# A selective-scan layer: shared products for B and C, paired input norm, centring folded into sums, and new rules for background work

## The chip, the core and the metric

The program runs on one core of a Trainium2 chip. A core has TensorE (PE, matrix products), VectorE (DVE), ScalarE (ACT), GpSimd (POOL) and a queue for DMA issues on SyncE (SP). The metric is the device time of one execution in microseconds (us); lower is better. A DMA moves data between HBM and the on-chip memory SBUF. PE writes to PSUM, a second on-chip memory of which this kernel gives two banks to small products.

## The reference, cut to what matters

Four layers follow one another; only the first is changed. It works on 8 images of 64 channels and 64 x 64 places. The part that matters:

```python
# x: (B, 64, 64, 64); DI = 128, N = 16, R = 4, K = 4 directions
xh = xh + _ss2d(_ln(xh, ln1_g, ln1_b), ...)      # norm over the 64 channels
xz = einsum(x, in_proj_w) + in_proj_b            # 64 -> 2 * 128
xi, z = split(xz, 2)
xc = silu(dwconv3(xi))                           # 3 x 3, per channel
xs = stack(rows of xc, columns of xc, both of them reversed)   # k = 0, 1, 2, 3
dts, Bs, Cs = split(einsum(xs, xproj_w), [R, R + N])
dts = softplus(dts through dtproj_w + dtproj_b)
h = h * exp(dt * A) + dt * B * u                 # for each of 16 n, along L = 4096
y_k = sum over n of h_n * C_n  + D * u
y = y_0 + y_1 + y_2 + y_3                        # put back in place
y = _ln(y, outnorm_g, outnorm_b) * silu(z)       # norm over the 128 channels
x = x + y through outproj_w
```

Directions 0 and 2 read the same places of xc, as do 1 and 3; they differ in their weights and in the direction of the scan.

## The kernel before, in words

**Steps and turns.** An image takes 16 steps: four directions by four chunks of 1024 places (`steps`, order k = 0, 2, 1, 3, for the last image 1, 3, 0, 2). A step takes 16 turns, one for each n, so 8 images make 2048 turns. In a turn, written out by hand under a manual schedule: ACT makes `a` (L628); DVE multiplies `z` by `dus` in PSUM (L673) and runs the scan (L677); POOL multiplies the scan's result with C into `ct` (L682); PE adds `ct` to the running sum in PSUM (`sum_up`, L719, a product with the identity), three turns behind. For n in `BY_POOL` = 0, 3, 6, 8 the product with B is made on POOL (L636) from a broadcast copy, and ACT copies it to PSUM (L643), so that DVE has only the scan. Otherwise PE spreads B over the partitions (`spread`, L646) from three bf16 parts. C, and B for four n, reach SBUF by broadcast DMAs of 512 KB (L624), issued one turn ahead for C, into five `ct` buffers.

**Step ends.** At turn 3 `begin_sum` (L710) starts the new step's sum with `u` or the stored `y`, at turn 7 two sums are made, and at turn 3 ACT copies the finished sum to `y` (`empty`, L692). For odd k the places are read in columns, so these reads are strided.

**Preparation of the next step** (`prepare`, `project`, `pieces`): for odd k ACT turns `u` into `ut` (L558); two products give B and C (`lower`, L514), ACT copies them (L522), a DMA stores them to HBM; two products give the step size (L532), with two ACT passes each (L540, L541); Exp and Ln follow at turns 6 and 7 (L546, L549), two additions and multiplications on POOL (L552, L571). B is fetched again, split in three bf16 parts by ACT and POOL (L585 to L595), stored, and loaded as `bs`. These seven `pieces` run at turns 7 to 13.

**Background.** All other work is cut in items, a pair (make, use): `before` takes one item in a turn and issues its PE part, `after` issues the rest one turn later. The queue holds, for image b: output norm and projection of image b - 1 (`after`), loads, input norm and projection of image b + 1 (`norm_items`, `before`), its gates (Silu of z, L406), and its convolutions (nine products for each block of 512 places, in seven items of which two are empty; L421, L430). The items of the next step go to the front of the queue. `before` takes nothing at turn 7, and for odd k at turn 4. At the last step of an image `bg.drain()` empties the queue; half of the next image's convolutions are held back (`rest`) and go in front of its first steps. In image 0 (`early`) and in the last three steps (`late`) up to three and two items go in a turn.

**Norms.** For each block of 512 places: a product with I - 1/p centres it (L296), ACT copies it back (L300) and squares it (L302), a product sums the squares (L309). The variances go through HBM to be spread over 128 partitions (fetch L326, root L329, reciprocal on DVE L332, back L337), a product spreads them (L346), DVE multiplies (L350), ACT applies gain and bias (L351). The input norm uses 64 partitions, the output norm 128.

Of the kernel before, what the change touches and what calls it, by code (L numbers as in the profile page):

```python
# [165 lines left out]
class Background:  # L166
# [4 lines left out]

    def __init__(self):
        self.queue, self.last, self.late = deque(), None, []

    def add(self, items, first=False):
        if first:
            self.queue.extendleft(reversed(items))
        else:
            self.queue.extend(items)
# [4 lines left out]
    def before(self, skip=False):  # L184
        self.now = None
        if self.queue and not skip:
            make, use = self.queue.popleft()
            self.now = (use, make() if make else None)
# [12 lines left out]

    def drain(self):
        while self.queue or self.last or self.late:
            self.before()
            self.after()


def scan_layer(cm, x_in, w, xh):

    tc, nc = cm.tc, cm.nc  # L210
    with ExitStack() as ctx:
# [9 lines left out]
        ln1_g, ln1_b = cm.column(w["ln1_g"], C, "ln1_g"), cm.column(w["ln1_b"], C, "ln1_b")  # L221
# [9 lines left out]
        win = cm.tile([C, 2, DI], "win")  # L231
        for i in range(2):
            through(win[:, i, :], w["in_proj_w"][i * DI : (i + 1) * DI])
        wout = cm.tile([DI, C], "wout")
        through(wout, w["outproj_w"])
        wx = cm.tile([DI, 4, R + 2 * N], "wx")
# [4 lines left out]
        for k in range(4):  # L241
            through(wx[:, k, :], w["xproj_w"][k])
# [24 lines left out]
        ln1 = cm.norm_consts(C, "ln1")  # L267
        lno = cm.norm_consts(DI, "lno")
# [16 lines left out]
        def norm_items(src, p, consts, g, b, blocks=range(NBK)):  # L285

            cen, avg = consts
            j0, nb = blocks[0], len(blocks)
            var = dr.tile([L], F32, name="vard", tag="vard")[: nb * BK]
            rs = dr.tile([L], F32, name="rsd", tag="rsd")[: nb * BK]  # L290
            sq, sm = {}, {}

            def centre(j):
                def make():
                    ps = bank("cps")
                    nc.tensor.matmul(ps[:p], cen, src[:, bass.ts(j, BK)], start=True, stop=True)  # L296
                    return ps

                def use(ps):
                    nc.scalar.copy(src[:, bass.ts(j, BK)], ps[:p])  # L300
                    sq[j] = work.tile([128, BK], F32, name="sq", tag="sq")
                    nc.scalar.activation(sq[j][:p], ps[:p], AF.Square)  # L302

                return make, use

            def variance(j):
                def make():
                    ps = bank("vps1")
                    nc.tensor.matmul(  # L309
                        ps[:1], avg[:, NBK - 1 : NBK], sq.pop(j)[:p], start=True, stop=True  # L310
                    )
                    return ps

                def use(ps):
                    t = work.tile([NBK, BK], F32, name="vrow", tag="rstd", bufs=1)
                    nc.scalar.copy(t[:1], ps[:1])
                    bg.later(lambda: nc.sync.dma_start(
                        var[bass.ts(j - j0, BK)].rearrange("(o n) -> o n", o=1), t[:1]
                    ))

                return make, use
# [17 lines left out]
            def apply(j):  # L339
                blk = bass.ts(j, BK)  # L340

                def make():
                    ps = bank("rps")

                    row = cm.ident[:nb, j - j0 : j - j0 + 1].to_broadcast([nb, p])
                    nc.tensor.matmul(ps[:p], row, sm["r"], start=True, stop=True)  # L346
                    return ps

                def use(ps):
                    nc.vector.tensor_tensor(src[:, blk], src[:, blk], ps[:p], ALU.mult)  # L350
                    nc.scalar.activation(src[:, blk], src[:, blk], AF.Identity, bias=b, scale=g)  # L351

                return make, use

            none = (None, None)
            out = [centre(j) for j in blocks[:2]]
            for j in blocks:
                out.append(variance(j))
                if j + 2 - j0 < nb:
                    out.append(centre(j + 2))  # L360
            out += [none, (None, fetch), none, (None, root), (None, invert), none, (None, back)]
            out += [none] + [apply(j) for j in blocks]
# [3 lines left out]
        FIRST = (range(3), range(3, 5), range(5, 8))  # L366

        def before(b):

            xn = io.tile([C, L], F32, name="xn", tag="xn", bufs=1)  # L370
# [6 lines left out]
            def load(j):  # L377
                return lambda _: nc.sync.dma_start(xn[:, bass.ts(j, BK)], xs[:, bass.ts(j, BK)])

            def project_in(j):  # L380
                def make():
                    ps = bank("xps")
                    nc.tensor.matmul(
                        ps, win[:, 0, :], xn[:, bass.ts(j, BK)], start=True, stop=True
                    )
# [10 lines left out]
            def gate(j):  # L396
                def make():
                    ps = bank("zps")
                    nc.tensor.matmul(
                        ps, win[:, 1, :], xn[:, bass.ts(j, BK)], start=True, stop=True  # L400
                    )
# [9 lines left out]
            def convolve(j):  # L411
# [17 lines left out]
                def use(_):  # L429
                    nc.scalar.activation(u[:, bass.ts(j, BK)], held[0], AF.Silu, bias=convb)  # L430

                if b == 0:
                    return [(part(0, 5), None), (part(5, 9), use)]
                if b == NB - 1:
                    return [
                        (part(0, 3), None), (part(3, 5), None), (part(5, 7), None),
                        (part(7, 9), use),
                    ]
                return [
                    (part(0, 2), None), (part(2, 4), None), (None, None), (part(4, 6), None),  # L440
                    (part(6, 8), None), (None, None), (part(8, 9), use),
                ]

            items = [[(None, load(j)) for j in range(NBK)]]
            for blocks in (FIRST if b == 0 else (range(NBK),)):
                items.append(norm_items(xn, C, ln1, ln1_g, ln1_b, blocks))
                items[-1] += [project_in(j) for j in blocks]
            return u, zd, items, [gate(j) for j in range(NBK)], [convolve(j) for j in range(NBK)]

        def after(b, y, zd, blocks=range(NBK)):  # L450
# [15 lines left out]
            def project_out(j):  # L466
# [7 lines left out]
                def use(po):  # L474
# [6 lines left out]
                    if j + 2 in blocks:  # L481
                        multiply(j + 2)
# [3 lines left out]
            def begin(_):  # L486
                for j in blocks[:2]:
                    multiply(j)

            items = norm_items(y, DI, lno, on_g, on_b, blocks)  # L490
            items.insert(-2, (None, lambda _: [load(j) for j in blocks[:3]]))
            items += [(None, begin), (None, None)]
            out = [[project_out(j), (None, None)] for j in blocks]
            return items + sum(out, [])[:-1]
# [8 lines left out]
        def project(u, k, c):  # L503
# [5 lines left out]
            bc = dr.tile([2 * N, CH], F32, name="bc", tag="bc")  # L509

            def lower(i):
                def make():
                    ps = bank("dps")
                    nc.tensor.matmul(  # L514
                        ps[: 2 * N].rearrange("p (a b) -> p a b", b=S), wx[:, k, R:],
# [4 lines left out]
                def use(ps):  # L520

                    nc.scalar.copy(e[: 2 * N, bass.ts(i, BK)], ps[: 2 * N])  # L522
                    bg.later(lambda: nc.sync.dma_start(
                        bc[:, bass.ts(i, BK)], e[: 2 * N, bass.ts(i, BK)]
# [31 lines left out]
            def turn():  # L556

                nc.scalar.copy(uo, ordered(u, k, c))  # L558
# [1467 lines left out]
```

## Time and profile before

| | us |
|---|---|
| three timed runs, median (lowest to highest) | 12572.19 (12557.06 to 12573.62) |
| the profiled execution | 12567.77 |
| its span, first to last instruction | 12566.0 |
| first scan starts, last scan starts | 98.2, 7255.1 |

So the changed layer takes the first 7260 us or so of the span. The starts of the scans (L677) in the trace give the time of each image: 955.2, 883.7, 880.7, 877.6, 879.2, 878.2, 903.4 and 901.3 us for images 0 to 7. The same starts give each step, as a mean over images 2 to 5:

| step | 0 | 1 | 2 | 3 | 4 | 5 | 6 | 7 |
|---|---|---|---|---|---|---|---|---|
| us | 58.6 | 53.8 | 51.8 | 51.8 | 54.3 | 58.1 | 53.6 | 52.3 |
| **step** | **8** | **9** | **10** | **11** | **12** | **13** | **14** | **15** |
| us | 51.9 | 55.6 | 53.7 | 56.0 | 59.3 | 55.7 | 55.7 | 56.8 |

A profile's busy time is the time in which an engine executes; an idle gap is put down to what ended last before it. In the views below `x` is a count, numbers after `|` are busy us, mean ns of one, and idle us ahead of it with its cause.

### The profile page before, as it was taken

To read this page: it belongs to the slowest core of one execution; us is meant where nothing else is said; L and a number is where in the kernel's file an instruction comes from. 1 tells how busy PE (TensorE), PEld (TensorE's weight loads), DVE (VectorE), ACT (ScalarE), POOL (GpSimd) and SP (SyncE) were. 2 spreads that over 40 slices of the span, in tenths; PEclk is the share of its full clock that TensorE was granted. 3 is DMA by queue.
4 is the path that set the end of the run, shared out by engine and by line. 5 is a ranking of instruction groups with operands and counts; after the bars stand their busy time and mean duration, and the time that the engine had idled before them with its cause. 6 is when DMAs were issued, how large, how long until landed. Compare 5 with 4: busy or idle time off the path is not lost. (4 is left out here: it accounts for less than half of the span.)

```text
span 12566.0 us, 122564 instructions
## 1 busy us (share of the span) xinstructions
PE 11561.6 (92%) x39403; PEld 4098.9 (33%) x39403; DVE 10385.0 (83%) x7362; ACT 7996.2 (64%) x10740; POOL 7424.1 (59%) x3638
## 2 busy tenths in 40 slices
PE   7899999999999999999998889999987778999999
PEld 2233233233232332332332222332324463333333
DVE  4999999999989999999899858768687685676767
ACT  4777677777776776777776536546456584555554
POOL 4999999999999999999899810000004490000000
PEclk8999999999999999999999989999998788999999
DMA  3666666666656656656566510000011110000000
GB/s 96 211 203 205 213 203 204 213 201 211 211 197 220 204 196 220 205 200 219 191 200 211 186 47 15 17 24 6 18 38 39 40 25 23 12 11 17 6 11 6
DMA packets 547044, 1562.30 MB, mean 124 GB/s; under 512 B 133040, under 2 KB 150096, under 8 KB 543824
## 3 DMA queue, kind: packets, MB, share of 16 engines
q1 hardware_dynamic: 546384, 1554.33, 37.6%
q8 instruction: 314, 5.14, 0.2%
q14 instruction: 346, 2.83, 0.1%
HBM read 1456.35 MB, written 88.87 MB: 123 GB/s over the span
## 5 line engine op out<-in xcount | busy, mean ns | idle before, releaser
L682 POOL TENSOR_TENSOR ct<-ct,h 128x1024 f32<-128x1024 f32 x2048 | 4796.0, 2359 | 456.2 <-DVE h L677 197.7
L719 PE MATMUL yps<-ct,ident 128*128 128x512 f32 x8192 | 4071.2, 626 | 4.6 <-POOL ct L682 4.6
L677 DVE TENSOR_TENSOR_SCAN h<-a,state,z 128x1024 f32<-128x1024 f32 x1536 | 3572.2, 2341 | 102.7 <-POOL ct L682 30.8
L1027 DVE TENSOR_TENSOR sum<-sum,ex 128x1024 f32<-128x1024 f32 x1920 | 2348.1, 1223 | 617.9 <-ACT ex L1020 481.2
L1020 ACT ACTIVATE ex<-sc 128x1024 f32<-128x1024 f32 x2048 | 1967.9, 1024 | 1359.8 <-PE sc L1015 1359.8
L628 ACT ACTIVATE a<-dt,amat 128x1024 f32<-128x1024 f32 x2048 | 2344.7, 1146 | 611.5 <-DVE h L677 606.9
L673 DVE TENSOR_TENSOR z<-z,e 128x1024 f32<-128x1024 f32 x1536 | 1866.5, 1215 | 391.1 <-PE z L646 240.2
L719 PEld LDWEIGHTS yps<-ct,ident 128*128 128x128 f32 x8192 | 1444.8, 192 | 2033.2 <-issue 1816.6
L1034 PE MATMUL av<-ex,v 128*64 128x512 f32 x8192 | 1950.0, 604 | 0.0
L1015 PE MATMUL sc<-q,k 16*128 16x512 f32 (+1 forms) x8192 | 1562.2, 623 | 4.2 <-ACT q L1008 3.1
L677 DVE TENSOR_TENSOR_SCAN h<-a,z 128x1024 f32<-128x1024 f32 x512 | 1162.7, 2282 | 101.6 <-ACT z L643 85.9
L646 PE MATMUL z<-bs,pick 48*128 48x512 bf16 x3072 | 941.6, 387 | 324.7 <-DVE h L677 290.0
L636 POOL TENSOR_TENSOR bt<-bt,e 128x1024 f32<-128x1024 f32 x512 | 1209.1, 2362 | 4.7 <-DMA bt<-bc 4.7
L1341 POOL TENSOR_TENSOR gt<-gt,pad 128x1024 f32<-128x1024 f32 x16 | 34.9, 2179 | 1572.0 <-ACT gt L1340 1492.7
L1034 PEld LDWEIGHTS av<-ex,v 128*64 128x64 f32 x8192 | 512.2, 136 | 1332.8 <-issue 1278.9
L1015 PEld LDWEIGHTS sc<-q,k 16*128 16x128 f32 (+1 forms) x8192 | 528.4, 184 | 1016.2 <-issue 977.3
L643 ACT COPY z<-bt 128x1024 f32<-128x1024 f32 x512 | 519.4, 1014 | 460.4 <-DVE h L677 237.7
L646 PEld LDWEIGHTS <-pick 48*128 48x128 bf16 x3072 | 180.1, 95 | 1592.7 <-issue 756.6
L421 PE MATMUL vps<-pad,convd 128*128 128x512 f32 x1152 | 540.6, 594 | 0.0
L1714 DVE RECIPROCAL r<-e 128x512 f32<-128x512 f32 x128 | 420.7, 3324 | 0.0
L1717 POOL TENSOR_TENSOR r<-r,half 128x512 f32<-128x512 f32 x128 | 162.6, 1270 | 361.6 <-issue 188.8
L664 ACT COPY state<-h 128x1 f32<-128x1 f32 x2048 | 359.4, 176 | 1.6 <-DVE h L677 1.6
(408 smaller groups left out, 10581.9 us busy)
## 6 DMA issues: line engine op xcount, KB each, us to landing
ct<-bc SPq DMA_DIRECT2D x2048, 512.0 KB
bt<-bc SPq DMA_DIRECT2D x512, 512.0 KB
x<-x SPq DMA_DIRECT2D x12, 2048.0 KB
bc<-e SPq DMA_DIRECT2D x256, 64.0 KB
zd<-z SPq DMA_DIRECT2D x64, 256.0 KB
z<-zd SPq DMA_DIRECT2D x64, 256.0 KB
x<-x SPq DMA_DIRECT2D x32, 512.0 KB
part<-x SPq DMA_DIRECT2D x128, 128.0 KB
```

The costliest lines, as they stand in the source:

```text
L421: nc.tensor.matmul(held[0].rearrange("p (r c) -> p r c", c=S), convd[:, t, :], pad[:, j * rows + dy : (j + 1) * rows + dy, dx : dx + S], s ...
L628: ctl["exp", n] = nc.scalar.activation(ctl["a", n], ctl["dt"], AF.Exp, scale=amat[:, ctl["k"], n : n + 1])
L636: nc.gpsimd.tensor_tensor(bt, bt, ctl["dus"], ALU.mult)
L646: nc.tensor.matmul(z[:, bass.ts(i, BK)], pick[:, n : n + 1].to_broadcast([3 * N, DI]), ctl["bs"][:, bass.ts(i, BK)], start=True, stop=True,)
L673: first = nc.vector.tensor_tensor(z, z, ctl["dus"], ALU.mult)
L677: nc.vector.tensor_tensor_scan(h[:, flip], a[:, flip], z[:, flip], 0.0 if state is None else state[:, n : n + 1], ALU.mult, ALU.add,)
L682: freed[at] = nc.gpsimd.tensor_tensor(ct, ct, h, ALU.mult)
L719: nc.tensor.matmul(ctl["ps"][:, bass.ts(i, BK)], cm.ident, ct[:, bass.ts(i, BK)], start=False, stop=(n == N - 1 and not ctl["turns"]),)
L1015: nc.tensor.matmul(sc[:, e, :], k[r : r + d, bass.ts(j, 128)], qs[i][r : r + d, :], start=True, stop=True,)
L1020: nc.scalar.activation(ex, sc, AF.Exp)
L1027: nc.vector.tensor_tensor(sums[i], sums[i], ex, ALU.add)
L1034: nc.tensor.matmul(avs[i][r, :], v[:, j, r], ex[:, e, :], start=(j == 0), stop=(j == TQ - 1))
```

## The change

- **B and C of two directions in one product.** `lower` is made only for k < 2, with 64 weight columns: those of k and of k + 2. Store, fetch and split handle both (tiles twice as wide); a step with k >= 2 only loads its `bs`.
- **Input norm of two blocks at once.** Even blocks lie on partitions 0 to 63 and odd ones on 64 to 127, so the norm has four pairs in place of eight blocks. `in_proj_w` is held twice.
- **Centring inside the sums.** From the last step of the third direction on, the running sum is made with I - 1/128 (`lno_cen`) in place of the identity, so `y` is stored centred and the output norm has no centring product or copy.
- **Convolutions one per step.** A convolution is a group of five items (four in image 7) without empty ones. In each step one group (two in image 6) may open when enough turns are left for it; its items alternate with the queue's. `finish` forces convolutions only where the next step needs them; the drain at the image's end and `rest` are gone.
- **Busy turns kept free.** At turns 3, 6, 7 and 8 no item with a product is taken.
- The output norm's multiplications (POOL) follow each block's `apply`, and its projections come without empty items between them. The turn of `u` for odd k is issued at the start of the step.

```diff
-    def before(self, skip=False):
+    def before(self, busy=False, slots=0):
         self.now = None
-        if self.queue and not skip:
-            make, use = self.queue.popleft()
+        src = None
+        if busy:
+            if not self.queue or self.queue[0][0]:
+                return
+        elif self.open:
+            if not self.first and (self.item or len(self.open) >= slots or not self.queue):
+                src = self.open
+        elif self.groups and self.credit and not self.first and slots >= len(self.groups[0]):
+            src = self.open = self.groups.popleft()
+            self.credit -= 1
+        if src is None and self.queue:
+            src = self.queue
+            self.first = max(0, self.first - 1)
+        self.item = src is not self.open
+        if src:
+            make, use = src.popleft()
             self.now = (use, make() if make else None)
...
+    def finish(self, b, count):
+
+        while self.done.get(b, NBK) < count:
+            self.credit = 1
+            self.before(slots=NBK)
+            self.after()
...
+            out = [centre(i) for i in pairs[:2]] + [none] * (2 - len(pairs[:2]))
+            for i in pairs:
+                out.append(variance(i))
+                if i + 2 in pairs:
+                    out.append(centre(i + 2))
+            out += chain
+            out += [apply(i) for i in pairs[:2]] + [none] * (2 - len(pairs[:2]))
+            for i in pairs:
+                out += [project_in(2 * i), project_in(2 * i + 1)]
+                if i + 2 in pairs:
+                    out.insert(-1, apply(i + 2))
...
+            out = [(None, lambda _: [square(j) for j in blocks[:2]]), none]
+            out += [variance(j) for j in blocks] + chain
+            out.insert(-2, (None, lambda _: [load(j) for j in blocks[:3]]))
+            out += [apply(j) for j in blocks[:2]]
...
-        FIRST = (range(3), range(3, 5), range(5, 8))
+        FIRST = (range(2), range(2, 3), range(3, 4))
...
-                return [
-                    (part(0, 2), None), (part(2, 4), None), (None, None), (part(4, 6), None),
-                    (part(6, 8), None), (None, None), (part(8, 9), use),
-                ]
+                cuts = (0, 5, 9) if b == 0 else (0, 3, 5, 7, 9) if b == NB - 1 else (0, 2, 4, 6, 8, 9)
+                parts = [(part(t0, t1), None) for t0, t1 in zip(cuts, cuts[1:])]
+                return parts[:-1] + [(parts[-1][0], use)]
...
-            items = [lower(0), lower(1), step_size(0), step_size(1)]
+            items = [step_size(0), step_size(1)]
+            if k < 2:
+                low["bc"] = dr.tile([2, 2 * N, CH], F32, name="bc", tag="bc", bufs=8)
+                items = [lower(0), lower(1)] + items
             if k % 2:
...
-                items.insert(0, (turn, None))
+                nc.scalar.copy(uo, ordered(u, k, c))
+                items.insert(0, none)
...
-            return [fetch, first, subtract, second, third, store, get]
+            return ([fetch, first, subtract, second, third, store] if ctl["k"] < 2 else []) + [get]
...
-                    ctl["ps"][:, bass.ts(i, BK)], cm.ident, ct[:, bass.ts(i, BK)],
+                    ctl["ps"][:, bass.ts(i, BK)], ctl["mat"], ct[:, bass.ts(i, BK)],
...
+            bg.finish(b, 2 * c + 2 if s < NCH and k == 0 else NBK)
...
+                mat=lno_cen if s >= 3 * NCH - 1 else cm.ident,
...
+                bg.done[b] = 0
+                bg.add([(None, lambda _: bg.groups.extend(deque(conv) for conv in convs))])
                 bg.add(gates)
-                now = NBK // 2 if b < NB - 1 else NBK
...
-                        bg.drain()
                         nxt = prepare(b + 1, 0)
-                        bg.add(sum(rest.pop(b + 1, []), []))
+                    bg.credit = 2 if b == NB - 2 else 1
+                    idle = () if early or late else (3, 6, 7, 8)
...
-                            skip = twice or (n == LAG + 2 and ctl["k"] % 2 == 1)
-                            bg.before(skip and not early and not late)
+                            bg.before(n in idle, slots)
```

## The prediction

> **What bounds it now.** I read the slices of the page first, then the groups of DVE and POOL in the window of images 2 to 5 (1937 to 5453 us), then the timeline at the turns that last too long.
>
> ```profile
> DVE  4999999999989999999899858768687685676767
> POOL 4999999999999999999899810000004490000000
> PEclk8999999999999999999999989999998788999999
> ```
>
> A slice is 314 us; the changed layer is the first 23. DVE and POOL are nine tenths busy or more there, so the layer is near two limits at once. The groups tell how far from each:
>
> ```profile
> L677 DVE TENSOR_TENSOR_SCAN h<-a,state,z 128x1024 f32<-128x1024 f32 x769 | 1788.2, 2341 | 41.4 <-POOL ct L682 19.0 <-ACT z L643 1.8
> L673 DVE TENSOR_TENSOR z<-z,e 128x1024 f32<-128x1024 f32 x768 | 933.2, 1215 | 157.1 <-PE z L646 105.2 <-POOL ct L682 16.1 <-ACT state L664 15.4
> ...
> L682 POOL TENSOR_TENSOR ct<-ct,h 128x1024 f32<-128x1024 f32 x1025 | 2400.6, 2361 | 158.8 <-DMA ct<-bc 86.2 <-DVE h L677 44.7 <-PE yps L719 11.6
> L464 POOL TENSOR_TENSOR z<-z,y 128x512 f32<-128x512 f32 x32 | 40.4, 1268 | 0.0
> ```
>
> In 3516 us DVE idles 41 + 157 + 30 (the scans without state) = 228 us, POOL 159 us. Per image of 879 us that is 57 and 40: POOL works 839 to 850 us (by union, or by the groups' sum). POOL is the floor, near 848. The largest cause on DVE is PE's late `z`; on POOL it is the late DMA of C, whose buffer is freed by PE's sums. So PE, which is in order, is late at certain turns. The step table says where: a clean step (step 2) takes 51.8 us, 16 of them 829, so 50 us of an image are excess. By steps: 0 and 1, 8.8; 4 to 6, 10.6; 9 and 10, 5.7; 11 and 12, 11.7; 13 to 15, 12.8; the rest 0.7. I placed the queue's items on the turns by counting. Steps 0, 1 and 13 to 15 hold the convolutions; 4 to 6 the output norm's `apply` (DVE) and multiplications (POOL); 9 and 10 the input norm's `apply`; 11 and 12 the gates. What such a turn looks like, step 13 of image 3, turns 3 and 4:
>
> ```profile
> 3539.35 0.57 ACT L522 COPY e<-dps 32x512 f32<-32x512 f32 x1
> ...
> 3539.97 1.13 PE L532 MATMUL tps<-ut,wst 128*128 128x512 f32 x2 [2.00 <-ACT e L522]
> ...
> 3540.93 3.59 PE L710 MATMUL yps<-y,ident 128*128 128x512 f32 x4
> ...
> 3544.45 0.95 PE L646 MATMUL z<-bs,pick 48*128 48x512 bf16 x2
> ...
> 3545.54 1.23 DVE L673 TENSOR_TENSOR z<-z,e 128x1024 f32<-128x1024 f32 x1 [3.26 <-PE z L646]
> ```
>
> The step-size product stands ahead of `begin_sum` and waits 2.00 us for ACT to free its bank; the strided start takes 3.59 us; `z` comes after both, and DVE loses 3.26 us. And the gates:
>
> ```profile
> 3460.36 1.28 ACT L406 ACT_TABLE_LOAD   x1
> ...
> 3461.66 0.69 ACT L406 ACTIVATE z<-zps,inb 128x512 f32<-128x512 f32 x1
> ...
> 3462.36 1.28 ACT L628 ACT_TABLE_LOAD   x1
> ...
> 3467.90 2.29 DVE L677 TENSOR_TENSOR_SCAN h<-a,z 128x1024 f32<-128x1024 f32 x1 [3.57 <-ACT z L643]
> ```
>
> Each gate costs ACT 1.28 + 0.69 + 1.28 = 3.25 us, eight in consecutive turns: ACT falls behind and DVE waits 3.57 us.
>
> **The change part by part**, for one of images 1 to 5.
>
> *Work removed.* PE: the input norm has 12 products in place of 24, the output norm 8 fewer, `lower` 16 in place of 32: 36 products of two instructions; twelve such instructions back to back take 5.42 us in the timeline, 0.45 each, so 32 us. ACT: 4 x (0.573 + 0.592 + 0.571 + 0.813) for the input norm, 8 x 0.576 centring copies, 16 x 0.571 copies of `lower`, and at most half of 9.5 of splitting: about 27 us. SP: six issues of some 0.35 us in eight steps, 17 us. None of these is on the path by itself; they shorten what PE and ACT have in front of `z`. On the path: DVE loses four `apply` of 0.654, 2.6 us. POOL's splitting (0.429 + 0.428 in 16 steps, 13.7 us) becomes eight times two of double width; on the line between 0.43 us for 128 elements and 2.36 for 1024 that is 0.70 each, 11.2: 2.5 us less, but 0.54 more in a step with k < 2.
>
> *Turn 3 kept free.* The product that stood ahead of `begin_sum` goes to turn 4. By the scans' starts turn 4 is above its floor of 3.5 us by 4.2 us in step 0, 3.1, 2.8 and 1.5 in 13 to 15: 11.6 of the 50. Next late there is the strided start itself (3.59 in a turn of 3.48, but without a sum), so some 0.5 stays at each: 9 gained.
>
> *Convolutions.* Now 21.6 us (steps 0, 1, 13 to 15) for eight, 11.6 of it the turn 4 just counted: 10 for the rest, 1.25 each. The empty items that let PE catch up are gone: a part of two taps is 4 x 0.45 = 1.8 us, a usual turn has 3.48 - 0.60 - 1.98 = 0.9 free on PE, so PE is 0.9 later with each part, up to 2.5 at turns 5 and 10, and then has free turns. Steps with k = 0 or 1 prepared have their parts from turn 10 on, alternating with gates; those with k = 3 prepared put two of them at turns 4 and 5, just where the `ct` buffers are shortest. Bounds: 0 (all inside the slack of two `z` banks) and 3.1 per convolution (the turn 4 above). I take 1.75, nearer the row of today's convolutions: 14 in all, plus 2 for the starts.
>
> *Gates.* They alternate with convolution parts, so ACT has two turns for 3.25 us. ACT is 2550 / 3516 busy, 40 us a step; less 27 / 16 and the mean gate share of 3.25, 35; a step with three gates or convolution ends has 35 + 9.8 = 45 of 51.8. The Trainium skill, "ScalarE: Activation LUTs", What ACT_TABLE_LOAD costs, speaks against it: every switch costs the load and a drain of about as much again, 2.66 us, and one should group by table set. By that a gate takes 6.0 and the step 53, a loss of 1.5 in each of three steps. The rows show the load at 1283 ns and the Silu 0.02 us behind it, so I take the trace: 11.7 becomes 4, bounds 1 and 12.
>
> *Norms.* The output norm's 10.6 stays: its eight `apply` and eight multiplications (8 x 1.268 on POOL) are the floor's own work, in steps 2 and 3 now. The waits added there: the multiplication stands in POOL's queue behind an ACT pass, with `ct` behind it, and the reload of `z` on SP waits for PE, with C behind it; both were there before, a turn earlier. The input norm's 5.7 halves to 2.9.
>
> *New weights.* `lno_cen` costs what the identity costs; accumulated before the norm it needs no further work. *The turn of `u`* (1.94 on ACT) moves from turn 0 to the step's start, ahead of the same decay: nothing; if ACT is late, PE's `lower` waits (4.1 us in four images today).
>
> Sum: 10.6 + 2.9 + 4 + 14 + 2 + 0.7 = 34; an image takes 829 + 34 = 863, 16 less than 879. Images 1 to 5: 5 x 16, and 4 for image 1, which is 4.6 above the others: **-84**.
>
> **The other images.** Image 6 (903.4): its steps 12 to 15 (63.7, 60.8, 62.8, 66.7) hold all eight convolutions of image 7 and the drain. By my count they now lie in steps 7 to 12, two each in 11 and 12. I give these 5 more each: 873, **-30**. Image 0: steps 0 and 1 (81.3 and 92.7) run two and three items a turn; with pairs both have two, so 92.7 becomes 81, and both lose some 4 for two fewer blocks; the rest 4: **-24**. Image 7: steps 13 to 15 (69.6, 74.9, 64.2) are 53 above clean.
>
> ```profile
> 7162.94 0.20 DVE L332 RECIPROCAL vsm<-vsm 128x8 f32<-128x8 f32 x1 [5.51 <-ACT vsm L329]
> ```
>
> This stall stays, as the round trip through HBM has the same turns. Centring and the next step's `lower` and splitting go: a third, **-17**. Start and end lose two small chains: **-6**. Total -161 from 12567.8: **12407 us**. The profiled execution lies 4.4 us under the median of the runs shown, which I neglect.
>
> The skill's "TensorE: Matmul & The Clock Gate", Part 1, is the other rule against it: after an idle window of about 3.4 us the clock falls to half, and this change makes PE idle. The window of the three late steps, with PE gaps of 5 to 6 us, shows a granted clock of 0.84; images 2 to 5 show 0.98. An idle turn leaves PE free for 0.9 us, far below the window, so I take 0.98. At half clock a turn's 2.58 us would be 5.2, a loss of 1.7 per turn.
>
> **Rivals.** (1) *POOL-bound*: all stalls vanish and images 1 to 5 sit at 850. For it: PE and ACT get 32 and 27 us. Against: parts at turns 4 and 5. -149 for these, -35, -50, -35 and -8 for the others: 12291. (2) *The wait comes back*: unbroken convolution parts make `z` and C late as before, 24 for eight, gates 8: an image gains 3 to 4; with -10, -15, -10, -9 elsewhere 12504. (3) *Slower*: PE runs more than two `z` banks late in every convolution step, and DVE stalls as at turn 4 above twice a step, 6.2 per convolution. My gain is used up at 161 / (8 x 7) = 2.9 over my 1.75, so 4.6 decides; at 6.2 it is 88 slower: 12656. For it: the pauses are gone; against: PE has 32 us less and the whole group ends two turns or more before most steps do. (4) *No effect*: POOL's own work falls by only 2.5 us an image; if its lag hides what PE gains, nothing moves: 12560.
>
> **Numbers.** Forecast 0.62, (1) 0.15, (2) 0.14, (3) 0.06, (4) 0.03. A change under 0.2% (25 us) can't be told from none here. Faster 0.91, same 0.03, slower 0.06. The range 12300 to 12500 takes in most of (1) and (2); the forecast's own is 12350 to 12460.
>
> **What would show it.** Right: DVE's idle for PE `z` under half of 105 us in four images; turn 4 of odd steps below 4.5 us; no DVE wait on ACT `z` of 3 us; image 6 within 15 of its neighbours; 128 `lower` instructions in four images in place of 256. Wrong: POOL's wait for the DMA of C above 86 us, stalls at turns 5 to 8 of steps 11 to 14, or a granted clock under 0.95 in these steps, where dense weights replace the identity.

## The result, and the profile after

| | before | after |
|---|---|---|
| timed runs on one chip, median (lowest to highest), us | 12567.08 (12557.06 to 12573.62) | 12475.58 (12474.25 to 12476.57) |
| the profiled execution: span, us | 12566.0 | 12472.4 |
| image 0, image 1 | 955.2, 883.7 | 939.4, 869.3 |
| images 2 to 5, mean | 878.9 | 867.9 |
| image 6, image 7 | 903.4, 901.3 | 880.0, 914.0 |

The ratio is 0.9928, with a 95% interval of 0.9911 to 0.9945: 91.5 us less, where 161 were forecast. The time lies in the stated range but above the forecast's own band (12350 to 12460), on the way to rival (2)'s 12504. Images 1 to 5 are 11.7 us shorter on average and image 7 is 12.7 us longer. The slices of the page of the changed kernel:

```profile
DVE  4999999999999999999989857768687785676767
POOL 4999999999999999999999800000005490000000
PEclk8999999999999999999989889999998789999999
```

A slice is 312 us. The 21st, 6236 to 6548 us, lies in image 7: DVE and the clock show 8 in it, in place of 9 in the slices ahead. The groups of VectorE in images 2 to 5 (busy us, mean ns | idle us ahead, with causes):

```profile
L768 DVE TENSOR_TENSOR_SCAN h<-a,state,z 128x1024 f32<-128x1024 f32 x768 | 1786.5, 2342 | 37.3 <-ACT z L734 9.3 <-POOL ct L773 7.5
L764 DVE TENSOR_TENSOR z<-z,e 128x1024 f32<-128x1024 f32 x768 | 932.9, 1215 | 120.1 <-PE z L737 79.4 <-POOL ct L773 12.1 <-ACT e L614 8.8
...
L450 DVE TENSOR_TENSOR y<-y,rps 128x512 f32<-128x512 f32 x32 | 21.2, 664 | 14.7 <-PE rps L445 14.7
```

The idle for PE's `z` fell from 105.2 to 79.4 us only, and a wait of 14.7 us stands where there was none: the output norm's `apply` (L450) waits for PE. Before, in the same four images, it was:

```profile
L350 DVE TENSOR_TENSOR y<-y,rps 128x512 f32<-128x512 f32 x32 | 21.2, 662 | 0.0
```

The same window of the changed kernel for POOL and for PE:

```profile
L773 POOL TENSOR_TENSOR ct<-ct,h 128x1024 f32<-128x1024 f32 x1025 | 2400.5, 2364 | 125.0 <-DMA ct<-bc 82.7 <-DVE h L768 20.7 <-PE z L737 6.3
```

```profile
L445 PE MATMUL rps<-rstd,ident 8*128 8x512 f32 x64 | 39.5, 699 | 26.3 <-DMA rstd<-rsd 26.3
```

POOL's wait for C is 82.7 us, before 86.2: nearly unchanged. PE now stands 26.3 us for `rstd`, the reciprocal roots that `back` fetches. PE's busy time in these four images fell from 3352.4 to 3236.9 us and ScalarE's from 2549.8 to 2458.6, so the work went about as counted. The steps, mean over images 2 to 5, from the scans' starts:

| step | 0 | 1 | 2 | 3 | 4 | 5 | 6 | 7 |
|---|---|---|---|---|---|---|---|---|
| us | 52.8 | 52.0 | 61.0 | 57.0 | 51.9 | 54.1 | 51.6 | 55.9 |
| **step** | **8** | **9** | **10** | **11** | **12** | **13** | **14** | **15** |
| us | 52.7 | 53.7 | 54.4 | 55.6 | 50.3 | 55.3 | 55.6 | 53.9 |

**Where step 2 loses.** Its turns 0 and 1 take 8.40 and 5.64 us in place of 3.5 each. The timeline of image 3 there (start us, us it took, engine, line; in brackets the idle time before it and what ended it; `SPq` issues a DMA):

```profile
2863.70 0.42 SPq L715 DMA_DIRECT2D ct<-bc  x1
...
2864.17 0.50 SPq L559 DMA_DIRECT2D xr<-in_x_dram  x1
2864.72 0.58 SPq L561 DMA_DIRECT2D z<-zd  x1
...
2867.34 0.32 SPq L561 DMA_DIRECT2D z<-zd  x1
...
2867.72 0.42 SPq L699 DMA_DIRECT2D bs<-bsd  x1
...
2868.36 0.33 SPq L715 DMA_DIRECT2D bt<-bc  x1
...
2869.07 0.32 SPq L715 DMA_DIRECT2D ct<-bc  x1
...
2870.15 0.29 SPq L356 DMA_DIRECT2D rstd<-rsd  x1
...
2876.82 2.04 PE L445 MATMUL rps<-rstd,ident 8*128 8x512 f32 x2 [6.52 <-DMA rstd<-rsd]
2878.79 1.03 PE L737 MATMUL z<-bs,pick 48*128 48x512 bf16 x2
...
2878.90 0.69 DVE L450 TENSOR_TENSOR y<-y,rps 128x512 f32<-128x512 f32 x1 [3.64 <-PE rps L445]
2879.75 2.93 PE L810 MATMUL yps<-ct,ident 128*128 128x512 f32 x3
```

The change put the loads of the first three blocks (three of `xr`, three of `z`) just ahead of `back`. They take SP from 2864.17 to 2867.66, `bs`, `bt` and C follow, and only then the small `rstd` goes out. It arrives 6.6 us after its issue, and PE stands 6.52 us for it; `z`, two turns of sums and the scans wait behind. What the wait does to the clock is in the same kernel's table by windows (us, busy of each engine with counts, granted clock, share of the DMA engines, GB/s):

```profile
2850.00:2870.00 20.00, 14.72 (x36) 4.70 (x34) 19.82 (x13) 11.28 (x19) 20.00 (x11) 1.00 0.66 197
2870.00:2877.00 7.00, 0.48 (x2) 0.21 (x2) 5.22 (x3) 3.41 (x5) 5.18 (x4) 0.78 1.04 325
2877.00:2885.00 8.00, 8.00 (x11) 1.99 (x12) 4.26 (x3) 2.00 (x4) 7.66 (x4) 0.55 0.32 125
```

While PE waits, the DMA engines are full (1.04, 325 GB/s): the small transfer shares them with the 512 KB ones issued before it. Whether their bytes or their place in the queue hold it up, the runs do not tell apart. And PE comes out of the wait at a clock of 0.55: two products of `z` take 1.03 us in place of 0.60. Turn 1 is long as well; how much of that is the clock, and how much the work that piled up, was not measured.

**Image 7** has the same queue two thirds into its step 2, and pays more. By windows:

```profile
6370.00:6398.00 28.00, 27.40 (x57) 8.59 (x56) 24.23 (x14) 21.10 (x28) 24.43 (x11) 0.95 0.60 181
6398.00:6403.00 5.00, 0.38 (x1) 0.41 (x2) 2.81 (x2) 1.92 (x4) 3.99 (x3) 0.70 1.05 361
6403.00:6427.00 24.00, 24.00 (x33) 6.24 (x33) 13.85 (x10) 8.54 (x15) 19.40 (x11) 0.57 0.35 114
```

PE idles about 5 us (second row), then works without a gap for 24 us at a mean of 0.57: turns 10 to 13 take 8.5, 6.7, 6.7 and 6.8 us, and step 2 takes 70.4 (53.1 before). The PE and ScalarE rows of this place:

```profile
6402.62 2.04 PE L445 MATMUL rps<-rstd,ident 8*128 8x512 f32 x2 [4.74 <-ACT state L755]
6404.59 1.03 PE L737 MATMUL z<-bs,pick 48*128 48x512 bf16 x2
6405.56 3.78 PE L810 MATMUL yps<-ct,ident 128*128 128x512 f32 x4
6409.27 2.07 PE L445 MATMUL rps<-rstd,ident 8*128 8x512 f32 x2
```

```profile
6401.09 0.40 ACT L677 CAST bp<-bw 128x256 bf16<-128x256 f32 x1 [4.36 <-DMA z<-zd]
```

The first row names ACT, whose small copy ended at that moment. By the trace PE's queue stood for the semaphore of `rstd` until 6402.5 us, 5.4 us after its issue at 6397.10. The products of an `apply`, those of `z` and four sums at half clock are 2.04 + 1.03 + 3.78 = 6.85 us, the turn's length. The split of B (L677) waits 4.36 us too: its fetch of `bw` was issued right behind the same loads.

### The profile page after: what moved, and what is told of

It is laid out like the page before. It is cut to its first block, busy times and chain, and to the rows that moved or that the text cites. A ratio compares the mean times of both kernels' runs of the same rounds, so it can differ in the third digit from the quotient of the medians.

```text
span 12472.4 us, 119759 instructions
## 1 busy us (share of the span) xinstructions
PE 11350.5 (91%) x38827; PEld 4100.1 (33%) x38827; DVE 10374.0 (83%) x7334; ACT 7820.0 (63%) x10296; POOL 7404.9 (59%) x3510
## 5 line engine op out<-in xcount | busy, mean ns | idle before, releaser
L810 PE MATMUL yps<-ct,ident 128*128 128x512 f32 x5632 | 2810.5, 629 | 6.9 <-POOL ct L773 6.8
L810 PEld LDWEIGHTS yps<-ct,ident 128*128 128x128 f32 x5632 | 1009.0, 194 | 1390.9 <-issue 1253.2
L810 PE MATMUL yps<-ct,lno_cen 128*128 128x512 f32 x2560 | 1313.1, 646 | 0.5 <-POOL ct L773 0.5
L810 PEld LDWEIGHTS yps<-ct,lno_cen 128*128 128x128 f32 x2560 | 468.6, 198 | 637.3 <-issue 560.7
```

What stands on the lines that cost most here:

```text
L810: nc.tensor.matmul(ctl["ps"][:, bass.ts(i, BK)], ctl["mat"], ct[:, bass.ts(i, BK)], start=False, stop=(n == N - 1 and not ctl["turns"]),)
```

## The experiments

Each is the changed kernel with the edit shown; ratios are to the kernel before on the same chip (changed kernel: 0.9928).

**Loads earlier.** The six loads are issued with the norm's first squares; an empty item takes their old place, so nothing else moves.

```diff
-            out = [(None, lambda _: [square(j) for j in blocks[:2]]), none]
+            out = [(None, lambda _: [square(j) for j in blocks[:2]]), (None, lambda _: [load(j) for j in blocks[:3]])]
...
-            out.insert(-2, (None, lambda _: [load(j) for j in blocks[:3]]))
+            out.insert(-2, none)
```

> The six loads of the output norm (x and gate, three blocks each) are issued with its first squares instead of just ahead of the DMA that brings the reciprocal root back. Theory A (the loads stand ahead of that DMA in SP's queue, and PE's first spreading product waits in order behind it): turns 0 and 1 of step 2, now 8.4 and 5.6 us, fall to about 3.5 each, so 7 us in each of images 1 to 6, and some 13 in image 7, whose step 2 takes 70.4 us: 12420 us, 50 to 60 below the changed kernel. Theory B (the wait is the round trip through HBM itself, which had the same length before): turns 0 and 1 stay above 7 us together by more than 5, and the time stays within 10 us.

Measured: 12418.01 us, ratio 0.9884 (0.9868 to 0.9901). Step 2 fell from 61.0 to 55.6, turns 0 and 1 to 4.08 and 3.92, step 2 of image 7 to 60.6. In images 2 to 5 PE's wait is:

```profile
L445 PE MATMUL rps<-rstd,ident 8*128 8x512 f32 x64 | 37.4, 664 | 5.1 <-DMA rstd<-rsd 5.1
```

5.1 us in place of 26.3: the loads ahead of `back` are the cause of this wait. The runs of this kernel spread over 48 us, and its profiled one is the longest: there, in images 2 to 5, other steps take the whole gain of step 2 back (868.7 us an image). So the 0.0044 rests on the median of four runs, not on that profile.

**Turns 4 and 5 free too**, in steps of odd k that prepare one with k = 3.

```diff
+                    if idle and nxt and ctl["k"] % 2 and nxt["k"] == 3:
+                        idle = (3, 4, 5, 6, 7, 8)
```

> In the odd steps that prepare k = 3, turns 4 and 5 take no product either, so that the convolution has its parts at turns 9 to 13. Theory A (two parts right behind the strided start of the sum are what makes z and C late): turn 6 of steps 11, 13 and 14, now 6.9, 6.0 and 6.8 us, falls to 3.5, and an image loses 8 to 9 us: 12415 to 12425 us. Theory B (a part is paid wherever it stands, and more free turns let PE's clock fall to half more often): the lateness moves to turns 9 to 14, PE's half-rate time grows above 614 us, and the time stays within 15 us of 12475 or rises.

Measured: 12409.47 us, ratio 0.9881 (0.9864 to 0.9897). What is removed is seen in the changed kernel at step 11 of image 3 (turns 4 to 6):

```profile
3385.46 2.15 PE L530 MATMUL vps<-pad,convd 128*128 128x512 f32 x4
...
3387.45 1.88 PE L810 MATMUL yps<-ct,lno_cen 128*128 128x512 f32 x4
...
3389.16 1.88 PE L530 MATMUL vps<-pad,convd 128*128 128x512 f32 x4
3389.66 2.35 POOL L773 TENSOR_TENSOR ct<-ct,h 128x1024 f32<-128x1024 f32 x1 [2.16 <-DMA ct<-bc]
...
3390.97 0.60 PE L737 MATMUL z<-bs,pick 48*128 48x512 bf16 x2
...
3391.78 1.23 DVE L764 TENSOR_TENSOR z<-z,e 128x1024 f32<-128x1024 f32 x1 [3.83 <-PE z L737]
```

Two parts of a convolution, 2.15 and 1.88 us, in turns that follow each other; `z` comes 3.83 us late for DVE and C's buffer 2.16 us late for POOL. Without them turn 6 of steps 11, 13 and 14 went from 6.90, 5.99 and 6.80 us to 4.00, 4.37 and 3.94. In the profile images 2 to 5 gained 5.2 us each, not the 8 to 9 expected; 17 us more lie in image 7, whose stalls differ much between these kernels. The wait for PE `z` in images 2 to 5 fell from 79.4 to 54.9:

```profile
L764 DVE TENSOR_TENSOR z<-z,e 128x1024 f32<-128x1024 f32 x768 | 933.1, 1215 | 104.5 <-PE z L737 54.9 <-POOL ct L773 16.3 <-ACT e L614 12.0
```

**Both together.** Both edits above.

> The loads of the output norm issued early (as in e1) and turns 4 and 5 free in the odd steps that prepare k = 3 (as in e2). If the two waits are separate, the gains add: 12345 to 12375 us, images 2 to 5 at 855 to 858. If the second is only what the first uncovers, or POOL's own 848 us an image is reached first, the time stays above 12390.

Measured: 12380.80 us, ratio 0.9847 (0.983 to 0.9863). Below the changed kernel by 0.0081 of the time before, where the two alone give 0.0044 and 0.0047: nearly the sum, as they repair different turns.

**No free turns.**

```diff
-                    idle = () if early or late else (3, 6, 7, 8)
+                    idle = ()
```

> The rule of free turns alone is taken back: every turn may take a product (turn 7 with its two sums too). Theory A (the product ahead of the sum's start costs a stall at turn 4): turn 4 of the odd steps and of step 0 is 2 to 3 us longer again, 60 to 90 us in all: 12535 to 12565. Theory C (free turns leave PE idle and cost clock): half-rate time falls to 500 us or less and the time changes by less than 20 us either way.

Measured: 12627.49 us, ratio 1.005 (1.0032 to 1.0068), slower than before the change and 0.0122 (about 153 us) above the changed kernel: more than expected. In step 10 of image 3, turn 8:

```profile
3436.57 2.31 PE L810 MATMUL yps<-ct,ident 128*128 128x512 f32 x5
...
3438.72 1.88 PE L530 MATMUL vps<-pad,convd 128*128 128x512 f32 x4
...
3440.53 0.60 PE L737 MATMUL z<-bs,pick 48*128 48x512 bf16 x2
...
3441.34 1.23 DVE L764 TENSOR_TENSOR z<-z,e 128x1024 f32<-128x1024 f32 x1 [3.46 <-PE z L737]
```

Turn 7 already makes two sums, and the part of a convolution after them makes `z` late by 3.46 us. Turn 8 takes 7.1 us on average in steps 7 to 10.

**The old free turns.** Only turn 7, and turn 4 for odd k, as before the change.

```diff
-                    idle = () if early or late else (3, 6, 7, 8)
+                    idle = () if early or late else (4, 7) if ctl["k"] % 2 else (7,)
```

> The rule of free turns of the kernel before in the changed kernel: turn 7 free, and turn 4 in odd steps; turns 3, 6 and 8 may take a product. In e4 most of the loss stood at turn 8, behind a product at turn 7 with its two sums. Theory A (turns 3, 6 and 8 are worth something too: the product ahead of the sum's start costs a stall at turn 4): 20 to 60 us above the changed kernel, 12495 to 12535, with turn 4 of odd steps or of step 0 longer by 2 us or more. Theory B (turn 7 alone counts): within 15 us of 12475.

Measured: 12518.91 us, ratio 0.9956 (0.9939 to 0.9973). So 3, 6 and 8 in place of 4 are worth 0.0028, about 35 us, though the two intervals overlap; turn 7, with 4 for odd k, makes the other 0.0094 of the run without free turns. The stalls moved to turns 3 and 8 (6.2 and 5.6 us at turn 3 in steps 10 and 8).

**A warm PE.** A product whose result nobody reads, at turns 5 and 15 when no background product is there.

```diff
-        self.now = None
+        self.now, self.product = None, False
...
+            self.product = bool(make)
...
+                        if n in (5, 15) and not bg.product and not early and not late:
+                            nc.tensor.matmul(
+                                bank("warm"), cm.ident, amat.rearrange("p k n -> p (k n)").unsqueeze(1).to_broadcast([DI, 8, 64]),
+                                start=True, stop=True,
+                            )
```

> One product that nobody reads is added on PE at turns 5 and 15 where no product of the background is made. Theory C (PE's idle gaps of 2.3 to 2.8 us at these turns let its clock fall to half, 614 us of half rate in the scan layer against 396 before the change, and this gives back part of the gain): half-rate time falls below 400 us, image 7 from 914 to below 905, and the whole time by 20 to 50 us. Theory D (half rate comes after the stalls, as their effect, and costs little): half-rate time falls but the time by less than 10 us, or it rises, as the added products stand in front of z.

Measured: 12471.11 us, ratio 0.9932 (0.9915 to 0.9949): no difference. The time at half clock in the changed layer, 614 us, fell to 580 only, so the run does not tell what the rest of it costs. The added product also takes one of the two small banks.

**The identity in all sums**, with the centring left out.

```diff
-                mat=lno_cen if s >= 3 * NCH - 1 else cm.ident,
+                mat=cm.ident,
```

> All sums are made with the identity, so that the mean over the 128 channels is not taken from y: the centring is left out. Theory A (the dense weights I - 1/128 cost what the identity costs; a sum's 640 against 623 ns lies in PE's slack): within 12 us of 12475, and the granted clock of steps 12 to 15 is the same within 0.01. Theory C (dense weights cost PE's clock): the clock of steps 12 to 15 rises by 0.02 or more and the time falls by 20 to 40 us.

Measured: 12461.14 us, ratio 0.9907 (0.9888 to 0.9927), overlapping the changed kernel's interval. Dense weights in five of sixteen steps cost nothing that can be told here, and no clock: in steps 12 to 15 of images 2 to 5 it was 0.934 with the identity, 0.950 in the changed kernel.

**B and C apart again**, a product, copy, store and split for each direction (`low` made anew in every step).

```diff
...
-            if k < 2:
-                low["bc"] = dr.tile([2, 2 * N, CH], F32, name="bc", tag="bc", bufs=8)
+            if True:
+                low["bc"] = dr.tile([1, 2 * N, CH], F32, name="bc", tag="bc", bufs=8)
...
-            return ([fetch, first, subtract, second, third, store] if ctl["k"] < 2 else []) + [get]
+            return [fetch, first, subtract, second, third, store, get]
...
```

> The changed kernel with one part undone: B and C of the two directions are formed by a product for each direction again, so per image 16 more products (about 14 us of TensorE), 16 more copies (about 9 us of ScalarE) and their DMA issues come back. Theory A (this work lies beside the path, which the turns of VectorE and GpSimd set): within 15 us of the changed kernel, a ratio of 0.992 to 0.994 to the kernel before. Theory B (every piece of TensorE's background work makes a scan's sum and then z late): +40 to +100 us, a ratio of 0.996 to 1.001.

Measured: 12408.96 us, ratio 0.9872 (0.9855 to 0.9888). Faster, which neither theory allows; the next run shows the same.

**The centring apart again**, eight products and eight copies back in the output norm.

```diff
...
-            out = [(None, lambda _: [square(j) for j in blocks[:2]]), none]
-            out += [variance(j) for j in blocks] + chain
+            out = [centre(j) for j in blocks[:2]]
+            for j in blocks:
+                out.append(variance(j))
+                if j + 2 in blocks:
+                    out.append(centre(j + 2))
+            out += chain
...
-                mat=lno_cen if s >= 3 * NCH - 1 else cm.ident,
+                mat=cm.ident,
```

> The changed kernel with one part undone: the output norm's mean is taken off by products and copies of its own again, and the scan's sums are formed with the identity. Per image 8 more products and 8 more copies come back, all in steps 12 to 15. Theory A (beside the path): within 15 us of the changed kernel, a ratio of 0.992 to 0.994 to the kernel before. Theory B (the norm's pieces lengthen the last steps of every image): +20 to +60 us, a ratio of 0.994 to 0.998.

Measured: 12407.38 us, ratio 0.9877 (0.986 to 0.9893). Neither theory again: with the removed work put back, the kernel is 64 to 70 us faster in these two runs. Step 2 of images 2 to 5 takes 54.6 us with B and C apart and 53.0 with the centring apart. In image 7 the run with B and C apart keeps the stall (step 2 takes 72.4 us). More items in the queue move all later ones, `back` among them, to other turns. Whether that is the reason, the next run tells.

**The places without the work.** The centring stays inside the sums, but the norm's sequence keeps the places of the centring products, as items that do nothing and, like a product, are not taken at the free turns.

```diff
-            out = [(None, lambda _: [square(j) for j in blocks[:2]]), none]
-            out += [variance(j) for j in blocks] + chain
+            hold = (lambda: None, lambda _: None)
+            out = [(lambda: None, lambda _: [square(j) for j in blocks[:2]]), hold]
+            for j in blocks:
+                out.append(variance(j))
+                if j + 2 in blocks:
+                    out.append(hold)
+            out += chain
```

> The changed kernel with the centring still inside the sums, but with places kept in the output norm's sequence where the centring products stood in the run with the centring apart: eight items that do no work, and like a product are not taken at turns 3, 6, 7 and 8. So all later items of the image fall on the turns of that run, with none of its 8 products and 8 copies. Theory A (which turns the items fall on sets the time, not how many products there are): as that run, a ratio of 0.986 to 0.990 to the kernel before, step 2 of images 2 to 5 at 53 to 55 us in place of 61. Theory B (the identity in the sums, or the products themselves, brought the gain of that run): as the changed kernel, 0.991 to 0.995, step 2 near 61.

Measured: 12405.91 us, ratio 0.9871 (0.9854 to 0.9888); step 2 takes 52.9 us, step 2 of image 7 52.5. Theory A. The groups of PE and of DVE in images 2 to 5:

```profile
L445 PE MATMUL rps<-rstd,ident 8*128 8x512 f32 x64 | 35.7, 638 | 1.9 <-DMA rstd<-rsd 1.9
```

```profile
L769 DVE TENSOR_TENSOR z<-z,e 128x1024 f32<-128x1024 f32 x768 | 932.5, 1214 | 96.3 <-PE z L742 56.8 <-POOL ct L778 10.0 <-ACT xo L584 6.2
```

And its timeline, at turns 11 to 14 of step 2 of image 3:

```profile
2889.74 0.50 SPq L564 DMA_DIRECT2D xr<-in_x_dram  x1
...
2892.60 0.58 SPq L566 DMA_DIRECT2D z<-zd  x1
...
2897.38 0.29 SPq L356 DMA_DIRECT2D rstd<-rsd  x1
...
2899.64 0.33 SPq L704 DMA_DIRECT2D bs<-bsd  x1
2900.02 0.41 SPq L720 DMA_DIRECT2D bt<-bc  x1
...
2901.07 1.09 PE L445 MATMUL rps<-rstd,ident 8*128 8x512 f32 x2 [1.00 <-DMA rstd<-rsd]
```

The same six loads stand ahead of `rstd`, but `bs` and `bt` of the next step's turn 0 now come after it: it is there 3.7 us after its issue, and PE waits 1.00 us in place of 6.52. In the 6.5 us ahead of `rstd` 1472 KB were issued, in the changed kernel 2784. So in these images the loads hurt where they meet the end of a step, and the changed kernel put them there by having fewer items. Image 7 is another case: its stall at turn 10 has `bw` and C behind the loads, and no step's end; with the places kept, steps 2 and 3 together take 115.3 us in place of 128.7.

The places move more than `back`. Images 2 to 5 gain 9.3 us each by this profile: step 2 gains 8.1, step 7 4.3 and step 5 2.4, while steps 4 and 15 lose 3.9 and 2.9. The convolutions begin a step later as well, at step 8 in place of 7.

**Convolutions at will.** The limit of one a step is lifted.

```diff
-                    bg.credit = 2 if b == NB - 2 else 1
+                    bg.credit = NBK
```

> The changed kernel with one part undone: the limit of one convolution a step is lifted, so that several may open in one step as the planner's due times ask. Theory A (a second convolution in a step costs some 4 us more than in a step of its own, as the double steps of image 6 did in the kernel before): +30 us or more, a ratio of 0.995 or more to the kernel before. Theory B (only the number of convolutions counts, not how they are spread): within 15 us of the changed kernel, a ratio of 0.992 to 0.994.

Measured: 12465.61 us, ratio 0.9917 (0.9901 to 0.9934). By the trace each step of images 3 and 6 holds as many products of convolutions as in the changed kernel: the turns left and the gates between them hold the convolutions to one a step (two in the two steps of image 6), not the limit. The run tells nothing of what a second one would cost.

**Both repairs, and a longer chain at the end.** The two first edits, and empty items in the chain of the last two blocks, where the round trip through HBM stalls image 7.

```diff
+            if nb == 2:
+                fetch, root, invert, back = [do for do in chain if do is not none]
+                chain = [none, fetch, none, none, none, root, none, invert, none, back, none]
```

> e7, and in the last steps of image 7 (two blocks at a time) the output norm's chain has five more empty items and one less ahead of its back load, so that root, reciprocal and the spreading products come one to two turns later. Theory A (there DVE's reciprocal and PE's spreading product wait in order for the round trip through HBM): turns 9 and 12 of steps 13 to 15, now 9.2, 9.0, 5.9 and 9.1, 10.7, 8.4 us, fall by 3 to 5 us each, 20 to 30 us under e7. Theory B (these steps are held by ACT and by SP's queue, and the wait moves to the next turn): within 10 us of e7.

Measured: 12374.82 us, ratio 0.9839 (0.9823 to 0.9856), the best of all: 1.6% under the kernel before and about 0.9% under the changed one. Steps 13 to 15 of image 7 went from 64.6, 69.0 and 60.1 us to 62.6, 61.6 and 55.0 in the profiles, but the timed intervals with and without the chain overlap.

## Why the prediction was half right

The direction held, and of the forecast's 161 us 91.5 came, by parts that partly cancel: that the number fell into the stated range is in part luck. What is missing, by the profiles: image 7 30 us, images 1 to 5 25, image 0 8, image 6 7.

**The step that failed**: "the reload of `z` on SP waits for PE, with C behind it; both were there before, a turn earlier", for the output norm, priced at nothing. The first three loads of `xr` and `z` were not where they had been: they had followed the first six `apply`s and now precede `back`, and I looked at who waits behind a load but not at what is sent after it. It costs turns 0 and 1 of step 2 4.9 + 2.1 = 7 us in each usual image and most of the 17.3 us by which step 2 of image 7 grew. Issuing them earlier gave 0.0044 of the time, some 55 us, back.

**The clock rule.** I set the Trainium skill's "TensorE: Matmul & The Clock Gate", Part 1, aside, because an idle turn frees PE for 0.9 us only, and took a clock of 0.98; images 2 to 5 had 0.97. The waits of images 3 and 7, and turns 3 and 4 of step 14 of image 3, by windows (columns as above):

```profile
2870.60:2874.00 3.40, 0.00 (x0) 0.00 (x0) 3.36 (x3) 2.64 (x4) 3.40 (x2) 1.00 1.05 267
6396.60:6400.00 3.40, 1.28 (x3) 0.21 (x2) 3.37 (x3) 0.12 (x2) 3.27 (x2) 0.99 1.08 286
6400.00:6402.60 2.60, 0.00 (x0) 0.01 (x1) 0.84 (x1) 1.51 (x4) 1.59 (x2) 0.50 1.03 394
6402.60:6423.90 21.30, 21.28 (x26) 5.67 (x26) 12.80 (x9) 7.26 (x13) 18.50 (x11) 0.50 0.30 100
3536.20:3539.60 3.40, 2.21 (x4) 0.62 (x5) 3.36 (x3) 3.40 (x5) 3.40 (x3) 1.00 0.60 188
3539.60:3546.40 6.80, 6.80 (x10) 2.20 (x9) 5.91 (x4) 3.82 (x6) 6.80 (x3) 0.50 0.00 0
```

In image 3 the clock fell at 2874.0 us, after 3.4 us of full idleness, as the rule says of an idle window. In image 7 it fell at 6400.0, 2.1 us into the wait, and came back only after 21.3 us of unbroken work. The last two rows show it halved after a stretch in which PE was busy for 2.21 of 3.40 us. So it was not right that short gaps leave the clock alone. Of the 101 stretches of half rate in the layer, 13 have a PE gap of 3.4 us or more in or across the 3.4 us ahead of them. In images 2 to 5 they make 232 us, and 116 of these begin at turns 3 and 4; before it was 38 of 133, with the old free turns 24 of 171. That keeping turns free costs clock is likely by this, but not shown: the layer's half-rate time is 502 us with the old free turns and 590 with none. For the wait I had even worked out 1.7 us a turn; measured was 3.2 in image 7, since the turns also hold an `apply`. Half-rate time in the layer rose from 396 to 614 us. How much of it costs time stays open: loads issued earlier gained without lowering it (625).

**Convolutions and gates** were right in sum and wrong in their parts, so the agreement is luck. Steps 7 to 14, which hold both, lie 19.1 us above eight clean ones of 51.8, against 14 + 2 + 4. In images 1 to 6 no wait of DVE for ACT's `z` reaches 2 us, where each image had one of 3.4 to 3.9. But the parts at turns 4 and 5, which I named as the place of danger and spread evenly at 1.75 us per convolution, cost 3.4, 2.5 and 3.3 us at turn 6 of three steps; keeping these turns free was worth some 59 us over the layer.

**Right**: the sizes of what was removed (PE 29 us an image, forecast 32; ScalarE 23, forecast 27); that the centring's work is not on the path (0.9877 with its products and copies, 0.9871 with their places alone); `lno_cen` at no cost; POOL's double-width splits at 0.68 us (0.70). Turn 4 of steps 13, 14 and 15 takes 4.65, 4.40 and 4.78 us, in place of 6.62, 6.28 and 4.95, and that of step 0 3.45 in place of 7.74; in steps 10 and 11 it is 0.6 longer. The new choice of free turns is worth about 35 us by its run; I had put some 60 on it, 9 an image. Image 6 lies 13.6 us above image 5. The output norm's steps 2 and 3 lie 14.4 us above clean, where 10.6 were forecast; without the stall it would be some 7, so one error hid part of the other.

**Image 7's late third**, forecast at -17: steps 13 to 15 gained 9.1, as the stall there stayed and only shrank.

Of the signs named, the wait for PE `z` (79.4, not under 53) and the stalls at turn 6 of steps 11 to 14 spoke against the forecast, and both shrank by moving items, not by removing work. The clock of steps 11 to 14 was 0.953 on average (0.966 before) and 0.938 in image 4, at the edge of the sign at 0.95.

**Open.** Which parts brought the 91.5 us is not settled. The free turns account for about 35; the paired input norm, the new spread of the convolutions and the missing drain were not undone one by one. The places kept by empty items were not tried together with turns 4 and 5 free. That the run with B and C apart gained by its shift as well is argued only, from its step 2.

## What to carry to other kernels

Where background work is dealt out to fixed turns, removing an item moves all that follow; count on which turn each critical small step lands, before pricing the work removed. Issue large loads well ahead of a small transfer that an engine waits for with other work behind it, or after it, and keep both away from a step's end where the next large transfers start. Work beside the path can be worth nothing by itself: here 8 products and copies per image came back at no cost that shows, and their empty places were worth 70 us.

## What the runs showed of the hardware

A transfer of `rstd` (16 KB) was there 3.7 us after its issue where 1472 KB had been issued on the same queue in the 6.5 us ahead of it (2897 us with the places kept). It took 6.6 us where 2784 KB had been (2870 us in the changed kernel, DMA engines at a share of 1.04).

The stretches of half clock in the changed layer are all multiples of 3.41 us long. After a PE wait of 6.5 us in image 3 the clock came back within 7.4 us of unbroken work; after one of 4.7 us in image 7 it stayed at half through 21.3 us of it. What makes this difference is open.
